# Two attention heads summed in one PSUM bank, one register load per expert tile, one gate transfer per pair of experts, and a new instruction order

## The chip, the cores and the metric

The kernel runs on one core of one Trainium2 chip. A core has five engines that run side by side, each through its own instruction stream: TensorE (PE, matrix products, with its weight loads shown as PEld), VectorE (DVE), ScalarE (ACT), GpSimd (POOL) and SyncE (SP), which here issues nearly all DMA transfers. Matrix products land in PSUM, eight banks of 512 fp32 numbers on each of 128 partitions; everything else on chip lies in SBUF. The metric is device time in microseconds (us) of one execution.

## The reference

Input x has 8 sequences of 512 tokens with 128 features, fp32. Four sublayers follow each other, each wrapped in a residual and a layer normalization without gain:

```python
x = _layernorm(x + _L0_attn_ref(x, ...))   # linear attention, 16 heads, plus an ELU feed forward
x = _layernorm(x + _L0_ffn_ref(x, ...))    # mixture of 8 experts of 64, every expert on every token, top-2 gates
x = _layernorm(x + _L1_attn_ref(x, ...))   # softmax attention, 16 heads of 8, rotary positions
x = _layernorm(x + _L1_ffn_ref(x, ...))    # mixture of 8 experts of 176 (top 2) plus one shared expert
```

The change touches the second, the third and the fourth. The heart of each:

```python
# second: gates of all 8 experts, zero except for the two best
h = gelu(einsum('bsd,edh->bseh', x, w1) + b1)
out = einsum('bse,bsed->bsd', gates, einsum('bseh,ehd->bsed', h, w2) + b2)
# third
attn = softmax(einsum('bhqd,bhkd->bhqk', q, k) / sqrt(8), axis=-1)
out = einsum('bhqk,bhkd->bhqd', attn, v)
# fourth
h = silu((einsum('td,edh->teh', xf, w1) + b1) * (einsum('td,edh->teh', xf, w3) + b3))
y = einsum('te,ted->td', rw, einsum('teh,ehd->ted', h, w2) + b2) + z    # z: the shared expert
```

## The kernel before, in words

**Recorded, then issued in a written order.** The kernel's code doesn't issue instructions as it runs. A recorder (`Schedule`) notes each operation as a numbered piece of work, with what it depends on; groups inside `nc.together()` are one piece. At the end `issue()` emits them in the order of a long tuple of numbers, `ORDER`. Every PSUM tile gets its bank from a string, `BANK_OF`. Each engine then runs its own instructions strictly in that order, and waits where a semaphore isn't there yet. Since an engine is in order, a wait holds up all that stands behind it; on SP this means that a DMA that waits for its data delays every DMA issued after it. The costs in the recorder's calls (such as 0.9, 2.0) are what an offline planner used when it made `ORDER`; they aren't instructions.

**The stages.** First `keys()` makes the sums of the linear attention over all batches (about the first 200 us). Then, batch by batch and interleaved over several batches: `linear_attention_and_ffn`, `first_mixture`, `softmax_attention`, and the last mixture. For the first six batches the last mixture is sorted: `sort` finds each token's two experts, and 8 indirect DMAs per batch (`scatter`, on POOL) put each token's row twice into a DRAM array, ordered by expert. `tiles` then walks over that array, `combine` fetches each token's two results with 8 indirect DMAs (`gather`, POOL). Batches 0 to 4 are one group, cut into 27 tiles of 256 rows; batch 5 is a group by itself, 15 tiles of 128 rows. Batches 6 and 7 run through `dense_mixture`, all experts on all tokens.

**Softmax attention (`softmax_attention`, L1306).** The 16 heads are split into j = 0..3 and g = 0..3, head 4g + j. For each j, and each quarter kt of the keys, `probabilities` computes the scores of four heads at once (L1330, four matmuls side by side in PE's rows) and two exponentials on ACT (L1336). `values` (L1340) then multiplies them by the values: four matmuls side by side in PE's columns (L1342), head g writing PSUM rows 32g to 32g+31. The stationary operand is a window of 32 columns of `vv`, where each head has 8 columns of values and one column of ones, which gives the softmax's denominator; what the window holds beyond these nine (columns of the next heads) ends in rows that nobody reads. After four kt the bank of j is complete: DVE copies it to SBUF (L1349), four transposes on PE bring it into token order (L1351, the helper is L770), DVE takes the reciprocals of the denominators into `rden` (L1354) and multiplies (L1355). This happens four times a batch, once for each j. `values` runs one step behind `probabilities`. `attention_output` follows, and a check of `rden` (L1376, L1377), which sends the kernel to a general path, not taken here, where a sum is out of range.

**Gates of the first mixture (`first_mixture`, L1168).** The gates, [8 experts, 512 tokens], go to DRAM (L1211) and come back spread over partitions: for each of four tiles c, 64 partitions have the gates of expert 2c and 64 those of 2c+1. The helper `spread` (L1041) issues one DMA per expert (L1047), so two a tile and 8 a batch. DVE multiplies the hidden values by them (L1226) ahead of the matmuls L1233.

**Tiles of the sorted mixture (`tiles`, L1770).** Which expert a tile belongs to, and which row it starts at, is known only at run time. DVE writes both for all tiles into a small integer array `listed`, experts in one row and first rows in the other. Per tile SP needs them three times: to fetch the expert's weights (L1684), to fetch the rows (L1689), and to store the result (L1696). Each time `number` (L1676) loads the number from SBUF into an SP register (L1677), and the DMA takes its address from it. The weights have a ring of three buffers, so the weights of a tile can be fetched once the tile three before it is done. The tile's work: transposes (L1818), three hidden matmuls (L1824), `gated` on ACT and DVE, the output matmuls (L1832), and DVE's L1837.

Small tiles come from `tiny`, most with two buffers in turn.

Of the kernel before, what the change touches and what calls it, by code (L numbers as in the profile page):

```python
# [31 lines left out]
ALU = mybir.AluOpType  # L32
# [3 lines left out]
P = 128  # L36
B, N, D = 8, 512, 128
NT = N // P
# [5 lines left out]
V1 = (H2 - 1) * (HD2 + 1) + 32  # L44
# [42 lines left out]
    1, 4, 45, 687, 47, 32, 54, 686, 0, 13, 3, 5, 10, 15, 69, 7, 679, 70, 2, 39, 72, 82, 71, 53, 18, 50, 55, 680,  # L87
    52, 73, 683, 49, 35, 684, 4504, 20, 27, 66, 34, 12, 9, 67, 30, 11, 81, 28, 68, 8, 74, 23, 41, 90, 6, 75, 126,
    46, 78, 48, 127, 83, 76, 77, 89, 80, 85, 91, 682, 128, 79, 129, 86, 98, 51, 87, 97, 84, 105, 106, 88, 99, 133,
    681, 92, 94, 134, 93, 135, 100, 17, 40, 138, 33, 1281, 96, 22, 101, 130, 102, 95, 137, 26, 103, 145, 139, 146,  # L90
    104, 142, 147, 140, 141, 107, 148, 192, 150, 193, 153, 144, 108, 194, 149, 16, 25, 42, 143, 177, 152, 176, 185,
    151, 178, 109, 110, 179, 112, 184, 154, 111, 186, 155, 113, 195, 180, 136, 156, 187, 181, 157, 189, 158, 159,
    182, 188, 161, 183, 196, 160, 190, 197, 162, 204, 191, 205, 173, 212, 163, 206, 164, 198, 65, 200, 199, 172,
    201, 209, 202, 166, 688, 203, 208, 174, 207, 165, 168, 211, 235, 210, 236, 167, 237, 243, 238, 244, 169, 245,
    213, 170, 214, 175, 171, 310, 215, 251, 216, 217, 246, 220, 240, 239, 252, 248, 242, 115, 114, 241, 247, 116,
    219, 255, 218, 256, 264, 257, 231, 263, 221, 258, 222, 265, 249, 223, 232, 225, 254, 271, 250, 259, 260, 233,
    267, 261, 268, 262, 227, 266, 272, 224, 294, 270, 226, 269, 295, 273, 229, 296, 303, 311, 302, 312, 228, 304,
    299, 230, 305, 298, 630, 297, 306, 661, 274, 24, 234, 275, 301, 38, 278, 253, 316, 29, 314, 279, 31, 21, 315,
    300, 43, 277, 19, 307, 631, 317, 313, 290, 324, 308, 14, 651, 323, 44, 309, 327, 632, 325, 654, 318, 660, 328,
    280, 643, 320, 326, 633, 291, 319, 370, 329, 638, 282, 321, 284, 292, 281, 283, 322, 285, 331, 276, 330, 355,  # L100
    286, 354, 363, 356, 362, 357, 371, 287, 372, 364, 288, 359, 365, 289, 430, 639, 358, 655, 634, 332, 293, 360,
    366, 333, 361, 334, 367, 335, 339, 383, 368, 635, 340, 689, 384, 37, 369, 647, 337, 375, 376, 385, 342, 338,
    341, 377, 350, 379, 378, 343, 386, 380, 351, 344, 336, 391, 374, 387, 381, 346, 56, 382, 685, 348, 352, 388,
    414, 390, 345, 389, 415, 347, 416, 422, 490, 663, 431, 636, 423, 650, 432, 659, 392, 353, 424, 393, 394, 349,
    419, 395, 417, 664, 399, 641, 418, 36, 425, 400, 646, 426, 421, 373, 436, 411, 427, 420, 435, 665, 396, 429,
    648, 443, 437, 428, 444, 397, 447, 445, 402, 398, 446, 401, 410, 440, 434, 451, 438, 439, 404, 441, 412, 452,
    403, 442, 448, 406, 449, 405, 450, 475, 453, 474, 407, 476, 482, 491, 483, 492, 454, 493, 484, 413, 666, 455,
    456, 477, 653, 645, 408, 657, 494, 479, 485, 409, 667, 478, 662, 460, 575, 487, 480, 652, 459, 486, 481, 458,
    471, 649, 495, 489, 457, 496, 503, 668, 488, 470, 504, 461, 505, 462, 497, 472, 500, 498, 507, 506, 464, 499,
    463, 501, 465, 502, 467, 511, 508, 466, 509, 534, 510, 535, 512, 542, 536, 513, 543, 514, 544, 468, 516, 539,  # L110
    545, 469, 546, 515, 537, 519, 547, 517, 538, 520, 473, 540, 118, 518, 531, 120, 541, 122, 124, 117, 119, 121,
    548, 123, 521, 125, 530, 550, 549, 523, 551, 522, 552, 553, 532, 525, 555, 554, 573, 559, 692, 558, 693, 557,
    524, 570, 533, 556, 697, 694, 569, 64, 526, 574, 595, 576, 583, 571, 527, 560, 695, 572, 584, 577, 528, 578,
    585, 696, 579, 529, 637, 580, 708, 669, 698, 707, 581, 699, 582, 728, 700, 709, 727, 710, 59, 586, 712, 587,
    729, 711, 588, 701, 562, 589, 713, 561, 590, 60, 730, 564, 690, 714, 747, 715, 748, 591, 749, 592, 716, 702,
    597, 600, 596, 593, 703, 131, 563, 594, 61, 565, 717, 62, 567, 63, 691, 132, 750, 566, 704, 57, 602, 568, 58,
    705, 706, 601, 605, 718, 751, 598, 723, 719, 720, 722, 599, 721, 731, 724, 732, 610, 725, 733, 603, 734, 604,
    735, 607, 606, 726, 736, 772, 752, 608, 737, 743, 753, 909, 742, 640, 612, 670, 744, 754, 738, 611, 745, 755,
    613, 615, 739, 614, 740, 741, 912, 756, 913, 776, 746, 773, 757, 762, 914, 763, 916, 764, 915, 917, 620, 758,
    765, 759, 777, 918, 910, 927, 642, 609, 760, 766, 928, 919, 761, 656, 621, 929, 920, 767, 433, 931, 774, 921,  # L120
    930, 658, 768, 922, 932, 769, 947, 933, 948, 934, 778, 935, 770, 949, 923, 936, 622, 771, 937, 775, 616, 779,
    950, 623, 617, 924, 968, 780, 925, 618, 781, 938, 967, 625, 619, 782, 926, 911, 951, 786, 783, 939, 943, 940,
    785, 941, 784, 969, 787, 942, 788, 789, 970, 952, 944, 791, 953, 796, 793, 954, 955, 792, 627, 798, 626, 794,
    797, 956, 799, 801, 628, 957, 795, 629, 800, 802, 803, 806, 790, 958, 808, 807, 804, 959, 809, 805, 822, 960,
    810, 961, 671, 962, 811, 945, 815, 814, 812, 813, 819, 816, 818, 817, 963, 820, 672, 821, 824, 673, 826, 964,
    825, 823, 830, 827, 971, 829, 828, 674, 831, 833, 972, 834, 837, 832, 838, 835, 836, 965, 839, 840, 675, 644,
    841, 946, 844, 973, 845, 676, 842, 1316, 843, 974, 966, 975, 846, 848, 982, 847, 677, 983, 849, 867, 984, 850,
    851, 869, 976, 868, 871, 993, 997, 977, 870, 873, 872, 852, 992, 874, 985, 996, 875, 853, 978, 854, 979, 858,
    1323, 1317, 855, 986, 980, 678, 856, 859, 1324, 981, 1320, 994, 1325, 1319, 857, 988, 860, 1321, 861, 987, 862,
    863, 1338, 989, 1322, 864, 990, 865, 1326, 866, 1327, 624, 1335, 991, 876, 1328, 998, 995, 1339, 877, 999,  # L130
    1000, 1001, 882, 1334, 1340, 1318, 1329, 880, 1336, 879, 883, 1337, 1355, 1354, 878, 1002, 1341, 886, 1006,
    1342, 1004, 885, 1003, 1005, 1007, 884, 1374, 1008, 1330, 1356, 1016, 887, 1343, 1021, 881, 1018, 1357, 1011,
    1344, 888, 1013, 1012, 889, 1331, 1017, 1009, 890, 1014, 1345, 891, 1023, 1332, 1015, 1346, 1019, 1304, 1010,
    1020, 1022, 1333, 1026, 892, 1028, 1349, 1347, 1027, 1375, 894, 896, 893, 895, 1350, 900, 898, 899, 897, 1376,
    901, 1358, 1348, 902, 1024, 903, 1029, 1025, 906, 1042, 905, 1377, 1351, 1030, 904, 1359, 907, 1031, 1244,
    1129, 1035, 1360, 1130, 1133, 1033, 1032, 1034, 1037, 1039, 1038, 1036, 1143, 1046, 1134, 1040, 1044, 1041,
    1045, 1131, 1043, 1144, 1135, 1352, 1047, 1137, 1051, 1145, 1055, 1361, 1049, 1147, 1132, 1378, 1053, 1050,
    1379, 1048, 1054, 1052, 1058, 1369, 1057, 1056, 1723, 1059, 1136, 1370, 1060, 1146, 1371, 1138, 1353, 1362,
    1372, 1148, 1399, 1363, 1061, 1139, 1727, 1065, 1364, 1064, 1373, 1141, 1063, 1400, 1726, 1380, 1062, 908,
    1066, 1728, 1404, 1403, 1149, 1068, 1067, 1365, 1151, 1087, 1150, 1729, 1091, 1140, 1088, 1089, 1152, 1092,  # L140
    1093, 1090, 1142, 1742, 1094, 1741, 1069, 1170, 1095, 1381, 1153, 1366, 1070, 1072, 1382, 1071, 1731, 1154,
    1367, 1073, 1368, 1730, 1074, 1390, 1075, 1078, 1076, 1389, 1079, 1077, 1383, 1080, 1081, 1082, 1083, 1391,
    1732, 1384, 1084, 1743, 1392, 1085, 1086, 1744, 1155, 1097, 1385, 1156, 1096, 1393, 1100, 1386, 1157, 1401,
    1158, 1733, 1387, 1724, 1734, 1099, 1159, 1161, 1103, 1388, 1160, 1171, 1162, 1098, 1163, 1395, 1105, 1394,
    1164, 1165, 1102, 1106, 1396, 1101, 1169, 1405, 1735, 1166, 1397, 1167, 1192, 1736, 1168, 1172, 1398, 1175,
# [446 lines left out]
def kernel(ctx: ExitStack, tc: tile.TileContext, i: dict, out: bass.AP):  # L592
# [120 lines left out]
    wqf = keep("wqf", [P, HM])  # L713
    rtT = keep("rtT", [P, 2 * E1])

    rdens = Ring([keep(f"rden{n}", [P, 4, NT, 4]) for n in range(2)])
    bad = keep("bad", [P, B])


# [19 lines left out]
    for v in vvs.places:  # L739
        nc.gpsimd.memset(v, 1.0)  # L740
# [1274 lines left out]
```

## Time and profile before

| what | value |
|---|---|
| device time, median of 9 runs (lowest to highest) | 1135.38 us (1130.17 to 1140.62) |
| the profiled execution, device time | 1133.91 us |
| its span in the profile | 1131.8 us, 17007 instructions |
| PE's granted clock, mean | 0.978 |
| eviction copies L1349 | 32 of 0.686 us |
| transposes of one 128x128 block, all of L770 | 320 |
| value matmuls L1342 | 1024 records of 128x32 by 128x512 |
| exponentials of the softmax L1336 | 256 of 1.026 us |
| loads of a number into an SP register L1677 | 126 |
| DMA issues L1047, SP | 100, of which 64 in the first mixture and 36 in the dense one |
| indirect DMAs on POOL L1662, L1670 | 48 and 48, about 1.0 us each |

The page's second part shows where each engine works, in 40 slices of 28.3 us (tenths of busy time; PEclk is the granted clock):

```profile
PE   7999999998888999998999999999899888789995
...
DVE  3866666787898856889677787577679765765785
```

PE's row is full nearly everywhere; the last quarter has the thinnest part. How to read the group lines in the rest of this document: line of the code, engine, operation, what it writes and reads, shapes, how often; then busy time in total and the mean of one in ns; then the engine's idle time just before these instructions, and what ended most of it.

### The profile page before, as it was taken

How to read it: one execution, taken by the hardware profiler on the slowest of the kernel's cores; microseconds unless marked ns; L12 is line 12 of the kernel's file. 1: busy time of each engine (PE TensorE's matmuls, PEld its weight loads, DVE VectorE, ACT ScalarE, POOL GpSimd, SP SyncE). 2: the span in 40 equal slices, each digit the busy share in tenths (PEclk: the TensorE clock that was granted, in tenths of full speed). 3: DMA queues.
4: the chain of work that ended last, by engine and by line, in shares of the span. 5: the costliest groups of instructions: out<-in, count | busy, mean ns of one | idle time of the engine just before them, and what ended most of it. 6: DMA issues, size and time to landing. Idle time of an engine off the chain costs nothing.

```text
span 1131.8 us, 17007 instructions
## 1 busy us (share of the span) xinstructions
PE 1042.1 (92%) x5753; PEld 594.7 (53%) x5753; DVE 824.9 (73%) x1977; ACT 716.3 (63%) x971; POOL 425.2 (38%) x382
## 2 busy tenths in 40 slices
PE   7999999998888999998999999999899888789995
PEld 4444444575565445565455554444587646453553
DVE  3866666787898856889677787577679765765785
ACT  2434445565546898646788777697566765678554
POOL 0232343133262623237653354354124212433463
PEclk9999999999999999999999999899899999899998
DMA  6114470252314321025232233131357855552532
GB/s 199 43 34 152 153 242 12 103 203 72 108 56 141 118 88 57 1 85 186 71 136 75 76 133 96 62 129 33 115 172 237 257 153 179 188 166 86 149 112 77
DMA packets 103374, 134.55 MB, mean 119 GB/s; under 512 B 19650, under 2 KB 60669, under 8 KB 103281
## 3 DMA queue, kind: packets, MB, share of 16 engines
q1 hardware_dynamic: 99905, 126.55, 35.3%
q0 software_dynamic: 3072, 6.30, 2.0%
q8 instruction: 47, 0.77, 0.3%
q10 hardware_dynamic: 304, 0.56, 0.2%
q14 instruction: 46, 0.38, 0.1%
HBM read 81.93 MB, written 54.43 MB: 120 GB/s over the span
## 4 chain that ended last, share of the span: by engine, by line
PE 67%; DVE 13%; ACT 8%; DMA 4%; issue 4%; POOL 1%; another core or an unknown queue 1%; SPq 1%; POOLq 0%; ACTq 0%; DVEq 0%
PE ps L1342 9%; PE ps L857 5%; PE ps L818 5%; PE ps L828 5%; PE ps L1330 4%; PE ps L1110 4%; PE ps L1072 4%; ACT scratch L1336 3%; PE ps L1062 3%; PE ps L770 3%; PE ps L1824 2%; PE ps L1233 2%; PE ps L1102 2%; PE ps L1832 2%; PE ps L1137 2%
## 5 line engine op out<-in xcount | busy, mean ns | idle before, releaser
L1336 ACT ACTIVATE scratch<-ps 128x1024 f32<-128x1024 f32 x256 | 248.6, 1026 | 68.5 <-PE ps L1330 60.7
L1342 PE MATMUL ps<-scratch,vv 128*32 128x512 f32 x1024 | 140.5, 608 | 0.9 <-ACT scratch L1336 0.9
L1086 POOL TENSOR_TENSOR scratch<-scratch 128x1024 f32<-128x1024 f32 x32 | 65.6, 2049 | 113.5 <-ACT scratch L1083 92.3
L1330 PE MATMUL ps<-qx,kx 32*128 32x512 f32 x512 | 73.4, 499 | 21.6 <-ACT scratch L1336 8.4
L823 ACT ACTIVATE scratch<-ps 128x1024 f32<-128x1024 f32 x32 | 32.4, 1021 | 77.6 <-PE ps L818 71.5
L1330 PEld LDWEIGHTS ps<-qx,kx 32*128 32x128 f32 x512 | 29.6, 183 | 90.7 <-ACT scratch L1336 34.8
L1110 PEld LDWEIGHTS ps<-scratch 128*128 128x128 f32 x512 | 60.3, 192 | 13.9 <-ACT scratch L1106 7.2
L1110 PE MATMUL ps<-scratch 128*128 128x128 f32 x512 | 64.4, 279 | 2.7 <-ACT scratch L1106 2.7
L1072 PE MATMUL ps<-wqf,scratch 128*128 128x512 f32 x128 | 65.8, 614 | 1.1 <-ACT scratch L1106 1.1
L1062 PE MATMUL ps<-wq,scratch 128*128 128x512 f32 x128 | 64.7, 617 | 2.0 <-ACT scratch L1067 1.2
L818 PE MATMUL ps<-scratch 128*128 128x512 f32 x128 | 62.5, 610 | 0.7 <-ACT scratch L810 0.4
L857 PE MATMUL ps<-scratch,x_sb 128*128 128x512 f32 x128 | 62.0, 597 | 0.0
L1670 POOL DMA_INDIRECT scratch<-x_d,slots x48 | 48.4, 1008 | 34.3 <-DVE scratch L1851 19.3
L828 PE MATMUL ps<-scratch 128*128 128x512 f32 x128 | 61.2, 598 | 0.0
L1017 POOL TENSOR_TENSOR f_ln_rs<-f_ln_ve,nhalf 128x4 f32<-128x4 f32 x24 | 26.5, 1102 | 89.5 <-DVE f_ln_ve L1015 57.2
L1824 PE MATMUL ps<-scratch 128*128 128x256 f32 (+1 forms) x252 | 54.7, 353 | 4.7 <-DMA scratch<-w_d 3.3
L1662 POOL DMA_INDIRECT x_d<-scratch,slots x48 | 49.1, 1023 | 22.2 <-DVE slots L1736 12.1
L825 DVE TENSOR_REDUCE scratch<-scratch 128x16 f32<-128x1024 f32 x32 | 38.2, 1213 | 25.7 <-ACT scratch L823 25.5
L770 PE MATMUL ps<-ident,scratch 128*128 128x128 f32 x224 | 38.2, 293 | 11.8 <-DVE scratch L1349 6.4
L1824 PEld LDWEIGHTS ps<-scratch 128*128 128x128 f32 x252 | 40.8, 194 | 15.6 <-issue 3.6
L1709 ACT ACTIVATE scratch<-scratch 128x512 f32<-128x512 f32 (+2 forms) x48 | 29.5, 615 | 28.8 <-DVE scratch L1706 14.7
L1106 ACT COPY scratch<-ps 128x1024 f32<-128x1024 f32 x32 | 32.5, 1015 | 23.4 <-PE ps L1102 22.0
(292 smaller groups left out, 2475.4 us busy)
## 6 DMA issues: line engine op xcount, KB each, us to landing
halves_d<-scratch SPq DMA_DIRECT2D x32, 512.0 KB
scratch<-w_d SPq DMA_DIRECT2D x42, 386.0 KB
x_d<-scratch SPq DMA_DIRECT2D x27, 512.0 KB
scratch<-g_d SPq DMA_DIRECT2D x68, 128.0 KB
kx<-halves_d SPq DMA_DIRECT2D x32, 256.0 KB
qx<-halves_d SPq DMA_DIRECT2D x32, 256.0 KB
scratch<-z_d SPq DMA_DIRECT2D x8, 520.0 KB
kvo_d<-scratch SPq DMA_DIRECT2D x8, 512.0 KB
```

Of the source, the lines that this page charges most:

```text
L770: nc.tensor.transpose(dst_ps[:, t * P : (t + 1) * P], src[:, t, :], ident)
L818: nc.tensor.matmul(kp_ps[:, a, :], xT[:, t * P : (t + 1) * P], wk[:, a * 512 : (a + 1) * 512], start=True, stop=True,)
L828: nc.tensor.matmul(dp_ps[:, a, :], xT[:, t * P : (t + 1) * P], wkf[:, a * 512 : (a + 1) * 512], start=True, stop=True,)
L857: nc.tensor.matmul(xp_ps[:, a, :], x_of(b)[:, t, :], ek[:, t, a * 512 : (a + 1) * 512], start=(t == 0), stop=(t == NT - 1),)
L1062: nc.tensor.matmul(qp[:, a, :], xT[:, t * P : (t + 1) * P], wq[:, a * 512 : (a + 1) * 512], start=True, stop=True,)
L1072: nc.tensor.matmul(dp[:, a, :], xT[:, t * P : (t + 1) * P], wqf[:, a * 512 : (a + 1) * 512], start=True, stop=True,)
L1086: nc.gpsimd.tensor_tensor(pr, eq, zr[:, 0:HM], ALU.mult)
L1110: nc.tensor.matmul(at_ps[:, 0:D], qnT[:, c, :], kvo[:, c, :], start=(c == 0), stop=(c == 7))
L1330: nc.tensor.matmul(halves[g // 2][:, g % 2, :], kx[quarter, kt * P : (kt + 1) * P], qx[quarter, :], start=True, stop=True, tile_position=( ...
L1336: nc.scalar.activation(pr[:, 2 * a : 2 * a + 2], sc, AF.Exp, scale=1.0 / math.sqrt(HD2))
L1342: nc.tensor.matmul(av[32 * g : 32 * g + 32, :], vv[:, kt, head_columns(4 * g + j)], pr[:, g, :], start=(kt == 0), stop=(kt == NT - 1), til ...
L1824: nc.tensor.matmul(to, w[:, c : c + P], xf, start=True, stop=True)
```

## The change

Five parts.

1. *Two heads in one bank.* Each pair of neighbouring heads (j even, j odd) has 27 columns of `vv`: values and ones of the first, nine zeros, values and ones of the second. The window of the even head begins at its values, that of the odd head nine columns ahead of its own, at the zeros. So the matmuls of the even head give rows 0 to 8 its sums and add zeros to rows 9 to 17, those of the odd head the other way round, and eight steps (two j, four kt) accumulate in one bank. Copy, transposes, reciprocal and multiplication come once per pair.
2. *One gate transfer per tile* of the first mixture: one DMA whose source has two rows, each read 64 times.
3. *One load per tile* of the sorted mixture: `listed` holds expert and first row side by side, one instruction loads both into SP registers, and the three DMAs of the tile use them. The rows are fetched first now, since that step loads the numbers; the weights come after it. The store begins with a no-op on SP.
4. *Fewer buffers*: `vv` is wider (216 columns a key tile in place of 167), and `rden`, `ln_st`, `lg`, `ge`, `cnt`, `base` and `listed` have one buffer in place of two.
5. *Order anew*: `ORDER` and `BANK_OF` are other numbers throughout. Not shown.

```diff
-V1 = (H2 - 1) * (HD2 + 1) + 32
+V1 = H2 // 2 * 3 * (HD2 + 1)
...
-    rdens = Ring([keep(f"rden{n}", [P, 4, NT, 4]) for n in range(2)])
+    rdens = Ring([keep("rden", [P, 2, NT * 4, 2])])
...
-    vvs = Ring([keep(f"vv{n}", [P, NT, V1]) for n in range(2)])
+    vvs = Ring([keep(f"vv{n}", [P, NT * V1 + 23]) for n in range(2)])
+    def by_pair(v):
+        return v[:, 0 : NT * V1].rearrange("p (t u a e) -> p t u a e", t=NT, a=3, e=HD2 + 1)
     for v in vvs.places:
-        nc.gpsimd.memset(v, 1.0)
+        nc.gpsimd.memset(v, 0.0)
+        for a in range(2):
+            nc.gpsimd.memset(by_pair(v)[:, :, :, 2 * a, HD2], 1.0)
...
         for c in range(FC):
             gr = tile2("e_t")
-            spread(gr, g1_d[b], c * P, M)
+            nc.sync.dma_start(gr, g1_d[b, 2 * c : 2 * c + 2].unsqueeze(1).to_broadcast([2, M, N]))
...
-    def head_columns(h):
-        return slice(h * (HD2 + 1), h * (HD2 + 1) + 32)
+    def head_columns(h, t, second=0):
+        at = t * V1 + h // 2 * 3 * (HD2 + 1) + (2 * (h % 2) - second) * (HD2 + 1)
+        return slice(at, at + 32)
...
-                        av[32 * g : 32 * g + 32, :], vv[:, kt, head_columns(4 * g + j)], pr[:, g, :],
-                        start=(kt == 0), stop=(kt == NT - 1), tile_position=(0, 32 * g),
+                        av[32 * g : 32 * g + 32, :], vv[:, head_columns(4 * g + j, kt, j % 2)], pr[:, g, :],
+                        start=(j % 2 == 0 and kt == 0), stop=(j % 2 == 1 and kt == NT - 1), tile_position=(0, 32 * g),
                     )
-            if kt < NT - 1:
+            if j % 2 == 0 or kt < NT - 1:
                 return
...
-            trv = tr.rearrange("p (t g e) -> p t g e", g=4, e=32)
-            rd = rden[:, j]
+            trv = tr.rearrange("p (t e) -> p t e", e=32)[:, :, 0 : 2 * (HD2 + 1)]
+            trv = trv.rearrange("p t (a e) -> p t a e", a=2)
+            rd = rden[:, j // 2]
             nc.vector.reciprocal(rd, trv[:, :, :, HD2])
             nc.vector.tensor_tensor(
-                at5[:, :, :, j, :], trv[:, :, :, 0:HD2],
-                rd.unsqueeze(3).to_broadcast([P, NT, 4, HD2]), ALU.mult,
+                at5[:, :, j // 2], trv[:, :, :, 0:HD2], rd.unsqueeze(3).to_broadcast([P, NT * 4, 2, HD2]), ALU.mult,
             )
...
-                if kt == 0:
+                if kt == 0 and j % 2 == 0:
                     av = psb("av", brief=False)
...
-    def fetch_tokens(group):
-        def go(x, rows_d, first):
+    def fetch_tokens(group, tile):
+        def go(x, rows_d, pair):
             r = ROWS[group]
-            inst = tc.nc.sync.dma_start(x, rows_d[bass.ds(number(first, SLOTS[group] - r), r)].rearrange("(t p) d -> p t d", p=P))
+            _, numbers[tile] = tc.nc.values_load_multi_w_load_instructions(
+                pair, engines=[mybir.EngineType.SP], min_val=0, max_val=SLOTS[group] - r,
+                skip_runtime_bounds_check_because="made of counts of tokens that add up to no more than the slots",
+            )
+            inst = tc.nc.sync.dma_start(x, rows_d[bass.ds(numbers[tile][1], r)].rearrange("(t p) d -> p t d", p=P))
             apart("fetch", group, inst, [("scatter", group)])
...
+    def store_tokens(group, tile):
+        def go(rows_d, y, _):
+            tc.nc.sync.nop()
...
-        listed = tiny("m", [P, 2, 5 * E2], "listed", 2, mybir.dt.int32)
-        nc.vector.tensor_scalar(listed[:, 0, 0:most], expert, float(E2 - 1), None, ALU.min)
-        nc.vector.tensor_scalar(listed[:, 1, 0:most], at, float(tr), None, ALU.mult)
+        listed = tiny("m", [P, 5 * E2, 2], "listed", 1, mybir.dt.int32)
+        nc.vector.tensor_scalar(listed[:, 0:most, 0], expert, float(E2 - 1), None, ALU.min)
+        nc.vector.tensor_scalar(listed[:, 0:most, 1], at, float(tr), None, ALU.mult)
...
-            nc.do("sync", fetch_weights, (w,), (w_d, which), 0.9, 2.0)
-            nc.do("sync", fetch_tokens(group), (x,), (rows_d, first), 0.9, 2.0, ("tiles", group))
+            nc.do("sync", fetch_tokens(group, tile), (x,), (rows_d, listed[0:1, j]), 0.95, 2.0, ("tiles", group))
+            nc.do("sync", fetch_weights(tile), (w,), (w_d, listed[0:1, j]), 0.5, 2.0)
+            nc.works[-1].before.add(tile)
```

## The prediction

> **What bounds the kernel now.** I read the page first: the share of the engines and the chain of waits.
>
> ```profile
> PE 1042.1 (92%) x5753; PEld 594.7 (53%) x5753; DVE 824.9 (73%) x1977; ACT 716.3 (63%) x971; POOL 425.2 (38%) x382
> ...
> PE 67%; DVE 13%; ACT 8%; DMA 4%; issue 4%; POOL 1%; another core or an unknown queue 1%; SPq 1%; POOLq 0%; ACTq 0%; DVEq 0%
> ```
>
> TensorE (PE) is busy for 92% of the span and is two thirds of the chain that ended last. DVE and ACT have a quarter to a third of the span to spare, and SP's queue is 1% of the chain. So an instruction taken from PE should shorten the run, and one taken from DVE or SP only where that engine is what PE waits for.
>
> Then the windows by stage, because a share of the whole mixes stages:
>
> ```profile
> 500.00:815.00 315.00, 300.58 (x1813) 160.24 (x1814) 230.01 (x623) 234.50 (x301) 150.24 (x160) 0.97 0.31 100
> 815.00:1010.00 195.00, 165.97 (x1081) 121.46 (x1080) 142.33 (x413) 125.12 (x215) 58.13 (x60) 0.96 0.64 196
> ```
>
> (Columns: stretch, length, busy PE, PEld, DVE, ACT, POOL, granted clock, DMA share, GB/s.) From 500 to 815 us PE stands still for only 14.4 us of 315. From 815 to 1010 us, where the 42 expert tiles run, it stands still for 29.0 of 195, and the DMA engines are twice as busy. PE sets the pace in the first, DMAs and SP share in it in the second.
>
> Third, the groups by line and shape (busy us, mean ns | idle time before, who ended it), for the lines that the change touches:
>
> ```profile
> L770 PE MATMUL ps<-ident,scratch 128*128 128x128 f32 x224 | 38.2, 293 | 11.8 <-DVE scratch L1349 6.4 <-ACT scratch L1026 3.4 <-issue 1.5
> L1226 DVE TENSOR_TENSOR scratch<-scratch 128x512 f32<-128x512 f32 x32 | 25.9, 824 | 12.1 <-DMA scratch<-g_d 9.0 <-issue 3.1
> L1349 DVE COPY scratch<-ps 128x512 f32<-128x512 f32 x32 | 22.0, 686 | 28.5 <-PE ps L1342 16.6 <-remote 9.3 <-issue 2.5
> L1837 DVE SCALAR_TENSOR_TENSOR scratch<-scratch,ps 128x256 f32<-128x256 f32 x27 | 11.2, 416 | 7.4 <-PE ps L1832 4.9 <-issue 2.1
> L1355 DVE TENSOR_TENSOR scratch<-ps,rden 128x128 f32<-128x128 f32 x32 | 9.0, 282 | 0.4
> L1354 DVE RECIPROCAL rden<-ps 128x16 f32<-128x16 f32 x32 | 8.0, 249 | 25.1 <-PE ps L770 18.9 <-PE ps L1330 6.2
> ```
>
> **Part 1, two heads in one bank.** The value matmuls (L1342) stay as many. What goes is every second eviction: 16 copies L1349, 16 groups of four transposes (L770 called from L1351), 16 reciprocals and 16 multiplications; the 16 that stay of the last two are twice as wide. One group in the timeline:
>
> ```profile
> 641.03 0.67 DVE L1349 COPY scratch<-ps 128x512 f32<-128x512 f32 x1
> ...
> 642.18 0.66 PE L770 MATMUL ps<-ident,scratch 128*128 128x128 f32 x4
> ...
> 642.77 0.16 PEld L1342 LDWEIGHTS ps<-scratch,vv 128*32 128x32 f32 x8 [0.17 <-issue]
> ```
>
> From the first transpose to PE's next instruction is 0.59 us: that, not the 293 ns that one transpose is shown to last, is what the group costs PE. I took this step for all 32 groups in the timeline: 17.5 us. The 16 groups of even j, which go, hold 9.0 us, and PE stood still 4.8 us just ahead of them (3.2 of it at 911, 1.2 at 558). PE term: at least 64 transposes x 0.109 us (the step inside a group) = 7.0; at most 9.0 + 4.8 = 13.8; I take 9.0, for most of that idle time ends with a stall that hits DVE and ACT too (below), and will fall on another instruction.
>
> On DVE: 16 x 0.686 = 11.0 of copies; multiplications 32 x 0.282 = 9.0 become 16 x 0.416 (L1837, the nearest row with 256 elements) = 6.7; reciprocals 8.0 become 4.0 to 8.0. Together 13 to 17 us. Hidden: DVE is 27% idle, and it counts only where PE waits for the copy, which is in the 13.8. If that cover were gone, all 17 would count. The wider multiplication makes the end of each batch's attention 0.13 us later, 8 x 0.13 = 1.1 at worst; nothing, since the halved work before it is worth more.
>
> The Trainium skill (TensorE: Matmul & The Clock Gate, Part 4: PE-mode transpose) gives about 275 ns for a 128x128 transpose inside a kernel; this trace's 293 ns of one agrees. By it the 64 would be worth 17.6 us, but the trace shows four overlapping in 0.59 us, and the measurement decides.
>
> **Part 2, gates of two experts by one transfer.** Per batch, 8 issues L1047 become 4. SP saves 32 x 0.53 us (their mean in the trace) = 17 us, if one issue of two rows costs what one of one row does; two would be the upper bound, and then nothing is saved. The bytes are the same (256 KB a tile). PE feels only the first tile of a batch, whose landing DVE L1226 waits for:
>
> ```profile
> 299.27 4.30 DMA scratch<-g_d
> ...
> 486.09 4.29 DMA scratch<-g_d
> ...
> 625.11 3.67 DMA scratch<-g_d
> ...
> 920.74 3.79 DMA scratch<-g_d
> ```
>
> Four of the eight batches have it on the chain. One issue less ahead of the second half of the tile is 0.53 each, so 4 x 0.53 = 2.1 at most on the chain as it stands; 0 to 4.2 for eight; I take 1.5.
>
> **Part 3, a tile's numbers read once.** SP ran 126 loads L1677, mean 0.311 us (median 0.272), 39.2 us; 42 stay. A load of two numbers isn't in the trace: between one load (0.272) and two (0.544), so 11.4 to 22.8 us stay and 16 to 28 go. [...] In 815 to 1010 us SP had 108 us of work (62.8 issuing, 34.7 in loads, 10.8 in register work) and 34.0 of waiting in 195. So it is not the bound, but it can be late, and lateness there is soon felt: from the issue of a tile's weights (L1684) to its first matmul (L1824) is 4.9 us in the median of 42, and a landing takes
>
> ```profile
> 881.36 4.01 DMA scratch<-w_d
> ...
> 909.85 3.52 another core or an unknown queue
> ...
> 958.30 5.82 another core or an unknown queue
> ...
> 1005.48 3.26 DMA scratch<-w_d
> ```
>
> 3.3 to 4.0. The two stretches of 3.5 and 5.8 us are of one kind: POOL runs eight indirect DMAs in a row, and DVE, ACT and PE stand still; in the second SP's instructions slow to 0.7 us apiece. Fewer SP instructions there may shorten them. Term: 0 to 9.3 us; I take 1.5, since nothing takes the POOL run away (96 indirect DMAs before and after).
>
> The Trainium skill (Runtime: NRT & Kernel Launch, Instruction fetch mechanics) speaks against this part: about 200 ns a register even in bulk, so one load of two numbers would cost two. By it SP would go from 126 x 0.2 to 84 x 0.2 and save 8.4 us, not 16 to 28. No row here shows a load of two.
>
> **Part 4, what waits anew.** A tile's tokens are now fetched ahead of its weights, since they bring the number; L1689 can wait for PE to free an x buffer (8.3 us in 5 cases), and behind it on SP stand the weights, and behind those PE. One buffer instead of two for several small tiles, rden and the list: all are written by DVE, mostly after DVE's own reads, and the list's 15 rewritten entries have been loaded long before. Nothing, 0 to 2 us. Zeros in vv: a slightly larger memset and four narrow ones on POOL at the start, where POOL is 38% busy; nothing.
>
> **Part 5, the order.** I compared the built programs. In PE's order, counted by the trace's own steps, the first tile matmul stands behind 701 us of PE work before and 696 after, the last value matmul behind 886 and 880, the end behind 944 and 937. It is the same plan with 7 us taken out, not a new one. Of 128 score groups, 49 had less than 2.5 us of other PE work (two exponentials and their handovers) before their values, now 43. So order anew is 0, with PE's idle time as its scale: a tenth of 76.8 us, 7.7 either way.
>
> **Sum** against the profiled execution: 9.0 + 1.5 + 1.5 = 12.0, so the span goes from 1131.8 to 1119.8. That execution took 1133.9 with what lies around the span, 1.5 under the median of the nine runs, 1135.4; from the median I forecast **1123.4 us**.
>
> **Rivals.**
> *A stall goes too.* The 9.3 us of the two unknown waits and the 4.8 ahead of the removed transposes vanish with the smaller SP load: 1123.4 - 7.8 - 4.8 = 1110.8. For: both lie where SP has most to do. Against: POOL's run of eight stays.
> *PE's time turns into waits.* PE is in order, ACT keeps 716 us of work, and L1330 already waits for L1336; if three quarters of the 12 return as waits for exponentials, 1132.4, no change that can be told. Against: PE has only 14 us of idle time in the 315 us where half of the attention lies.
> *Slower: weights late.* With tokens ahead, each tile's weights are issued later. The slack is 4.9 - 4.0 = 0.9 us; from there on each tile pays. At 1.5 us later, 42 x 0.6 = 25, less 12: 1148.6; it decides from 1.2 us on (42 x 0.3 = 12.6). For: L1824 waits for w_d now (3.3 us). Against: in the new order tokens stand two to four tiles ahead, and SP has two loads a tile fewer.
>
> **How the numbers follow.** A measurement of this kernel can tell about 0.3% (3.4 us) from no change. Forecast 0.56, both stalls 0.14, waits 0.13, slower 0.17. Faster is 0.56 + 0.14 = 0.70, same 0.13, slower 0.17. Range: all terms at their upper bounds, 13.8 + 4.2 + 7.4 = 25.4, give 1110; on the other side into the slower rival as far as 1138, which leaves out its larger half and a few hundredths below. The forecast's own range is 1115 to 1131 (7.7 either way).
>
> **What would show it.** L770 with 64 fewer, L1349 and L1354 at 16, PE's busy time 9 to 18 us less (it counts the shown lengths), the chain's g_d pieces about 0.5 us shorter, SP's loads at 42 with a mean between 0.27 and 0.54, and the issue-to-matmul time of tiles still near 4.9. I'd be wrong if PE's idle time grew by as much as its work shrank, or if L1824 waited for w_d in many tiles.

## Result and profile after

The changed kernel takes 1246.1 us (median of 20 runs, 1239.6 to 1253.6) where the kernel before takes 1133.8 (62 runs): 1.0999 of before, with a 95% interval of 1.0977 to 1.1021. It is slower by 10%, and the prediction had 1123.4.

The page of the changed kernel: the span, the engines, and then, of the picture in 40 slices, PE and its granted clock (here as below, "..." stands for lines left out).

```profile
span 1244.9 us, 16659 instructions
...
PE 1066.5 (86%) x5689; PEld 605.5 (49%) x5689; DVE 804.4 (65%) x1929; ACT 715.2 (57%) x971; POOL 429.2 (34%) x386
...
PE   8999999985876999587799699599859987878995
...
PEclk9999999998898999898899699899889996999998
```

The work is what the change says: PE has 64 instructions fewer (5753 before), DVE 48 fewer (1977). The span grew by 113.1 us. PE's time outside its work went from 1131.8 - 1042.1 = 89.7 to 1244.9 - 1066.5 = 178.4, so 88.7 of the 113.1 are PE's idle time. The other 24.4 are work that lasts longer although it is less of it: the mean granted clock fell from 0.978 to 0.931, and most of PE's dips in the picture have dips of the clock beneath them.

Next the groups by line and shape, those that answer to the prediction's (busy us, mean ns | idle before, who ended it):

```profile
L771 PE MATMUL ps<-ident,scratch 128*128 128x128 f32 x160 | 26.9, 290 | 12.1 <-ACT scratch L1027 6.5 <-DVE scratch L1349 5.2 <-issue 0.4
...
L1227 DVE TENSOR_TENSOR scratch<-scratch 128x512 f32<-128x512 f32 x32 | 21.9, 691 | 137.8 <-DMA scratch<-g_d 137.8
...
L1349 DVE COPY scratch<-ps 128x512 f32<-128x512 f32 x16 | 11.0, 685 | 16.2 <-PE ps L1342 11.4 <-remote 4.6
...
L1356 DVE TENSOR_TENSOR scratch<-ps,rden 128x256 f32<-128x256 f32 x16 | 6.7, 420 | 0.3
...
L1355 DVE RECIPROCAL rden<-ps 128x32 f32<-128x32 f32 x16 | 5.7, 353 | 3.6 <-PE ps L771 3.0 <-ACT scratch L1336 0.6
```

Everything that the removed evictions should change has changed. What stands out is L1227, the multiplication by the gates (L1226 before): it waited 9.0 us for the gates and now waits 137.8. The waits say how often, and who stands behind it (waiter <- awaited: us, times, longest):

```profile
DVE scratch L1227 <- DMA scratch<-g_d: 137.8, 27, 9.1
...
PEld ps L1234 <- DVE scratch L1227: 29.0, 8, 9.9
PE ps L1234 <- DVE scratch L1227: 27.2, 8, 9.7
...
POOL scratch L1173 <- DVE scratch L1227: 24.1, 1, 24.1
...
PE ps L1063 <- DVE scratch L1083: 19.1, 2, 14.3
```

DVE waits for 27 of the 32 gate tiles, 5 us each in the mean. In one batch, the timeline (start, length, engine, line):

```profile
510.25 0.29 SPq L1212 DMA_DIRECT2D g_d<-gT  x1
...
511.73 3.85 SPq L1226 DMA_DIRECT2D scratch<-g_d  x3
...
515.68 5.48 SPq L1869 DMA_DIRECT2D scratch<-xT_d  x1
519.36 0.69 DVE L1227 TENSOR_TENSOR scratch<-scratch 128x512 f32<-128x512 f32 x1 [3.72 <-DMA scratch<-g_d]
...
521.82 0.58 SPq L1226 DMA_DIRECT2D scratch<-g_d  x1
524.71 0.69 DVE L1227 TENSOR_TENSOR scratch<-scratch 128x512 f32<-128x512 f32 x1 [4.66 <-DMA scratch<-g_d]
...
530.75 3.75 PE L1063 MATMUL ps<-wq,scratch 128*128 128x512 f32 x4 [14.67 <-DMA scratch<-xT_d]
...
536.67 0.69 DVE L1227 TENSOR_TENSOR scratch<-scratch 128x512 f32<-128x512 f32 x1 [8.71 <-DMA scratch<-g_d]
```

Three tiles are issued between 511.7 and 515.6, the fourth at 521.8. The first two are used at 519.4 and 524.7; the multiplication at 536.7 waits on the semaphore of the fourth, and the third, which landed at 530.0, is used after it, at 537.6. The transfer that follows the first three on SP, xT_d, takes 5.48 us to issue, and PE stands still for 14.67 us until it has landed. The DMA view of 508 to 535 us, in 40 slices of 0.675 us, says why (busy share of the 16 engines in tenths, then GB/s):

```profile
DMA  0000100011111111111177931111111111128411
GB/s 0 0 0 0 24 0 0 21 49 52 52 52 49 52 33 24 49 55 49 52 115 240 382 137 52 49 49 49 52 52 49 49 49 49 55 88 243 170 55 49
```

While gates alone move, the row shows one tenth of the engines busy and mostly 49 to 52 GB/s. The packets, counted one by one in these stretches, are about 25 a microsecond, of 2 KB and 84 ns each: 25 x 0.084 = 2.1 engines. So 256 KB take 5.2 us, and four tiles 21 us one behind the other. The semaphores say the same: besides one update a microsecond after the issue, the trace has two landings for a gate tile (519.26 and 519.27 us for the first one), and it has sixteen for xT_d, 14 of them by 523.8 us and the last two at 530.6, behind the gates. The peak in the middle is xT_d and a write to xs_d, issued at 521.3, on the other engines.

Summed over the eight batches, it was 48.1 us from the first to the fourth multiplication before, and it is 143.6 now.

### The profile page after: what moved, and what is told of

Same layout as the page of the kernel before. It is cut to its first block, busy times and chain, and to the rows that moved or that the text cites. A ratio compares the mean times of both kernels' runs of the same rounds, so it can differ in the third digit from the quotient of the medians.

```text
span 1244.9 us, 16659 instructions
## 1 busy us (share of the span) xinstructions
PE 1066.5 (86%) x5689; PEld 605.5 (49%) x5689; DVE 804.4 (65%) x1929; ACT 715.2 (57%) x971; POOL 429.2 (34%) x386
## 5 line engine op out<-in xcount | busy, mean ns | idle before, releaser
L1336 ACT ACTIVATE scratch<-ps 128x1024 f32<-128x1024 f32 x256 | 248.7, 1027 | 101.4 <-PE ps L1330 90.8
L1342 PE MATMUL ps<-scratch,vv 128*32 128x512 f32 x1024 | 145.9, 630 | 2.3 <-ACT scratch L1336 1.4
L1227 DVE TENSOR_TENSOR scratch<-scratch 128x512 f32<-128x512 f32 x32 | 21.9, 691 | 137.8 <-DMA scratch<-g_d 137.8
L1063 PE MATMUL ps<-wq,scratch 128*128 128x512 f32 x128 | 69.9, 653 | 35.3 <-DVE scratch L1083 19.1
L824 ACT ACTIVATE scratch<-ps 128x1024 f32<-128x1024 f32 x32 | 32.6, 1021 | 76.7 <-PE ps L819 72.7
L1111 PEld LDWEIGHTS ps<-scratch 128*128 128x128 f32 x512 | 61.3, 193 | 15.3 <-issue 6.9
L1234 PE MATMUL ps<-mw,scratch 128*128 128x128 f32 x256 | 44.7, 324 | 27.2 <-DVE scratch L1227 27.2
L1830 PE MATMUL ps<-scratch 128*128 128x256 f32 (+1 forms) x252 | 57.5, 367 | 2.0 <-DMA scratch<-w_d 1.6
L1670 POOL DMA_INDIRECT scratch<-x_d,slots x48 | 49.3, 1027 | 26.0 <-issue 11.1
L1068 ACT ACTIVATE scratch<-ps 128x1024 f32<-128x1024 f32 x32 | 32.7, 1023 | 38.0 <-PE ps L1063 38.0
L1234 PEld LDWEIGHTS ps<-mw,scratch 128*128 128x128 f32 x256 | 40.3, 235 | 29.0 <-DVE scratch L1227 29.0
```

The lines of the kernel that those rows point to most:

```text
L1063: nc.tensor.matmul(qp[:, a, :], xT[:, t * P : (t + 1) * P], wq[:, a * 512 : (a + 1) * 512], start=True, stop=True,)
L1111: nc.tensor.matmul(at_ps[:, 0:D], qnT[:, c, :], kvo[:, c, :], start=(c == 0), stop=(c == 7))
L1234: nc.tensor.matmul(op[:, sl], hT[:, c, t * P : (t + 1) * P], mw2[:, c, :], start=False, stop=(c == FC - 1),)
L1336: nc.scalar.activation(pr[:, 2 * a : 2 * a + 2], sc, AF.Exp, scale=1.0 / math.sqrt(HD2))
L1342: nc.tensor.matmul(av[32 * g : 32 * g + 32, :], vv[:, head_columns(4 * g + j, kt, j % 2)], pr[:, g, :], start=(j % 2 == 0 and kt == 0), st ...
L1830: nc.tensor.matmul(to, w[:, c : c + P], xf, start=True, stop=True)
```

## Experiments

Each run was compared with the kernel before on its own chip. There were three chips. Before takes 1104.1 us beside the first run with two transfers, each tile fetched twice, two copies and eight copies; 1128.4 beside the second run with two transfers, the evictions twice, three loads and half the evictions; 1130.4 beside the other four. So ratios are compared, and times in the expectations are to be read against 1133.8. The ratios with their 95% intervals are not the quotients of these medians; for the runs near 1 the two differ by up to 0.0014, or 1.6 us.

**Two transfers a tile in the new order.**

```diff
-            nc.sync.dma_start(gr, g1_d[b, 2 * c : 2 * c + 2].unsqueeze(1).to_broadcast([2, M, N]))
+            with nc.together():
+                for a in range(2):
+                    nc.sync.dma_start(gr[a * M : (a + 1) * M, :], g1_d[b, 2 * c + a].partition_broadcast(M))
```

> The changed kernel, but each gate tile is fetched by two transfers of 64 partitions in the place of the one of 2 x 64; order, banks, buffers and everything else stay. Theory A (few engines): the one transfer runs on two DMA engines. In the changed kernel's trace the DMA engines move 25 packets of 2 KB a microsecond, 84 ns each, while only such a transfer runs: 25 x 0.084 = 2.1 engines, 50 GB/s, so 256 KB take 5.2 us, and four tiles 21 us one behind the other. With two transfers the time falls to 1115 to 1135 us (the sum of the prediction gives 1123), the four multiplications of a batch spread over 5 to 8 us instead of 13.5 to 20.3, and DVE waits for g_d 5 to 20 us in all instead of 137.8. Theory B (the order, the single buffers or the tokens ahead of the weights are at fault, and the wait for the gates is only where it shows): 1230 to 1255 us.

1101.6 us against 1104.1: 0.9972 (0.9943 to 1.0001). The spread of a batch's four multiplications is 5.3 to 8.0 us, 54.2 in all. The group by line, with its mean, shows the wait gone:

```profile
L1229 DVE TENSOR_TENSOR scratch<-scratch 128x512 f32<-128x512 f32 x32 | 22.5, 713 | 16.3 <-DMA scratch<-g_d 12.5 <-ACT scratch L1338 3.8
```

137.8 us have become 12.5, by this edit alone. The order, the single buffers and the tokens ahead of the weights are all still in this kernel, so theory B falls.

**One transfer a tile in the order of before.** The two works of a tile in the order of before are meant to share one function (`gates_once`, not shown): the first to be issued is to fetch the whole tile, and the second to do nothing.

```diff
-            spread(gr, g1_d[b], c * P, M)
+            for a in range(2):
+                nc.do("sync", gates_once(gr), (gr[a * M : (a + 1) * M, :],), (g1_d[b, 2 * c : 2 * c + 2],), 0.6, 2.0)
```

> The kernel before, its order and banks, with the gate tile fetched by one transfer of 2 x 64 partitions in the place of the first of its two; the second becomes a no-operation. Theory A (few engines): the whole loss appears here too: the first-to-fourth multiplication of eight batches took 48.0 us before and 143.6 after, 96 us more, and the span grew by 113; so 1215 to 1250 us. Theory B (order, buffers, tokens first): 1130 to 1140 us, as before.

1.3123 (1.3076 to 1.3170): far beyond both. The edit did not do what the expectation says. The function was made anew for each work, so neither knew of the other and both fetched the tile: eight transfers of 256 KB a batch on two engines. It is a run with the suspected cost doubled, and the wait shows it: 352.4 us at the multiplication, 302.5 from first to fourth. Done as meant, with one function for both works (`once = gates_once(gr)` ahead of the inner loop, and `once` in its place):

> The kernel before, in its order, with the gate tile fetched by one transfer of 2 x 64 partitions. In the earlier run of this edit both works issued the transfer, so each tile was fetched twice on two engines (512 KB a tile) and the time was 1.31 of before; here the second work is a no-operation. Theory A (two engines, order not at fault): 256 KB a tile at 50 GB/s as in the changed kernel, so about its loss without the gain of the other parts: 1.08 to 1.14 of before. Theory B (the new order or the single buffers have a share in the loss): below 1.06.

1.1037 (1.0984 to 1.1089), inside theory A's range, and no different from the whole change's 1.0999. Page and waits of this run:

```profile
PE 1081.8 (87%) x5753; PEld 621.2 (50%) x5753; DVE 820.6 (66%) x1977; ACT 717.0 (57%) x971; POOL 423.3 (34%) x382
...
DVE scratch L1239 <- DMA scratch<-g_d: 127.1, 28, 10.0
```

PE and DVE have all the instructions of before, and the wait is there. The one transfer is enough for the whole loss.

**One transfer with more rows in its source.** The gates are written to DRAM two or eight times over, so that a tile's source is 4 rows for 32 partitions each, or 16 rows for 8 each; still one transfer, the same bytes and packets. The edit for two:

```diff
-    g1_d = tc.dram_tile([B, E1, N], F32, name="g1_d")
+    g1_d = tc.dram_tile([B, E1, 2, N], F32, name="g1_d")
...
-        nc.sync.dma_start(g1_d[b], gT1[0:E1])
+        nc.sync.dma_start(g1_d[b], gT1[0:E1].unsqueeze(1).to_broadcast([E1, 2, N]))
...
-            nc.sync.dma_start(gr, g1_d[b, 2 * c : 2 * c + 2].unsqueeze(1).to_broadcast([2, M, N]))
+            rows_of = g1_d[b, 2 * c : 2 * c + 2].rearrange("e k n -> (e k) n")
+            nc.sync.dma_start(gr, rows_of.unsqueeze(1).to_broadcast([4, 32, N]))
```

> The changed kernel, still one transfer a tile, but the gates are written to DRAM twice over (32 KB instead of 16), so that a tile's source is 4 rows, each spread over 32 partitions: the same 256 KB and the same 128 packets of 2 KB. Theory A, if the number of engines is that of the outermost rows: four engines, 100 GB/s, 2.6 us a tile, 10.5 us for four; most of the stall goes, 1125 to 1175 us, and the packets run at 50 a microsecond. Theory C (one transfer that spreads several rows is slow whatever its outermost count): 1235 to 1255 us, 25 packets a microsecond.

> As the run with two copies, with eight: the gates are written eight times over (128 KB instead of 16), and a tile's source is 16 rows, each spread over 8 partitions. Theory A: all 16 engines, so 1115 to 1140 us, as with two transfers, less one issue of about 0.5 us a tile and plus a longer write of the gates ahead of them. Theory C: 1235 to 1255 us.

Two copies: 1.0387 (1.0341 to 1.0433), a little above theory A's upper end (1175 / 1133.8 = 1.036). Eight copies: 1.0147 (1.0120 to 1.0174), above its end of 1.005. With two copies, the DMA view from 280 to 310 us, where the gates follow one another from 290 us on (slices of 0.75 us):

```profile
DMA  7303887000002002223994222222222200000000
GB/s 311 115 0 111 316 273 16 0 0 0 0 14 30 0 0 66 98 101 126 319 287 117 87 98 98 98 112 101 93 90 104 87 14 0 0 0 0 0 0 0
```

Twice the engines and about twice the rate, 87 to 117 GB/s where gates alone move: four engines for four rows. Here too the landings in the trace agree: four for a gate tile with two copies, sixteen with eight copies, sixteen for each half with two transfers. In one table, with the sum over eight batches from the first to the fourth multiplication, and that from the issue of the gates' write to the first multiplication:

| kernel | rows of a tile's source | first to fourth, us | write to first, us | ratio to before |
|---|---|---|---|---|
| before | 2 transfers, 64 partitions each | 48.1 | 49.8 | 1 |
| two transfers, new order | the same | 54.2 | 49.3 | 0.9972 |
| eight copies | 16 | 53.3 | 66.9 | 1.0147 |
| two copies | 4 | 85.0 | 68.8 | 1.0387 |
| changed | 2 | 143.6 | 82.7 | 1.0999 |

Theory C falls: it is not that one transfer serves two experts, but how many rows stand outermost. With 16 rows the tiles follow one another as fast as with two transfers. What eight copies still lose is in the fourth column, (66.9 - 49.3) / 8 = 2.2 us a batch ahead of the first tile. There the kernel writes 128 KB instead of 16, and the first gate transfer, which needs that write, is issued 4.5 us behind the issue of the write instead of 1.5 (medians of eight batches); the expectation had allowed too little for the write.

The Trainium skill says this outright (DMA: Bandwidth & Descriptors, Why a DMA increments its semaphore by 16 and not by 1): a transfer runs on the largest number of engines up to 16 that divides the slowest dimension, other than 1, of both its sides. Its Rules for kernel authors add that an outermost dimension of c below 16, a leading broadcast for example, confines the transfer to at most c engines. The runs agree for 2, 4 and 16 rows by the number of landings, for 2 and 4 also by the rates, and for 16 by the spread of the multiplications.

**What the other parts are worth.** With the gates mended, 3 us of gain are left where the prediction's other terms add up to 10.5. The two-transfer kernel was run again, beside three others.

> The kernel of the run with two transfers a tile once more, beside the next three, so that they are compared with it on one chip. It was 0.9972 of the kernel before, 3.1 us faster, with an interval that just touches no change. The prediction's sum without its term for the gates is 12.0 - 1.5 = 10.5 us. Theory P (the removed evictions are worth their 9, and the new order takes most of it back) and theory Q (the removed evictions were worth little, the order nothing) both expect 0.994 to 1.000 again; below 0.992 the sum would stand and the first run was low.

0.9949 (0.9920 to 0.9979): 1128.4 x 0.0051 = 5.8 us. Both runs of this kernel together lie near 4.5.

In the next, the removed evictions' work is done again in the kernel with two transfers: copies and transposes twice, reciprocals and multiplications in two halves (the halves are not shown).

```diff
-            nc.vector.tensor_copy(avs, av)
+            with nc.together():
+                for _ in range(2):
+                    nc.vector.tensor_copy(avs, av)
...
-            transpose4(tr, tok(avs))
+            with nc.together():
+                for n in range(2 * NT):
+                    t = n % NT
+                    nc.tensor.transpose(tr[:, t * P : (t + 1) * P], tok(avs)[:, t, :], ident)
```

> The kernel with two transfers a tile, in which each pair of heads is copied out of its bank twice, transposed twice, and its reciprocals and multiplications are done in two halves: 16 copies, 64 transposes, 16 reciprocals and 16 multiplications more, as many as the change removed. Theory P: 9 us more than the run with two transfers (7 to 14), so 1.003 to 1.010 of the kernel before. Theory Q: 0 to 4 us more, so 0.996 to 1.002.

1.0093 (1.0056 to 1.0130), 0.0144 or 16 us above the run before. Theory P's 7 to 14 lies below that, though within the intervals; theory Q's 0 to 4 does not. The doubled work is also not where the removed work was: each second copy stands between a pair's last value matmul and its transposes. With the second edit of that diff alone, the transposes:

> The kernel with two transfers a tile, with the 16 groups of four transposes done twice, 64 transposes more on PE and nothing else. The prediction's PE term: 9.0 us (7.0 by the step inside a group) above the kernel with two transfers, so 1.001 to 1.006 of before. If the removed transposes lay beside other waits: 0 to 4 us, 0.995 to 1.000. The run with all evictions' work again was 16 us above it; what is left of that is the copies and the other work on DVE.

0.9998 (0.9967 to 1.0029). Above the two runs of the two-transfer kernel (0.9972, 0.9949) that is 2.9 and 5.5 us, so 64 transposes are worth some 4 us, less than the 7.0 of the step inside a group; with the intervals, 7 is not excluded, nor, against the first of the two runs, is nothing. By subtraction, which no run of its own shows, the other 12 of the 16 us are the doubled DVE work, where it was put.

The same part taken out of the kernel before (the wider multiplication is not shown), in its own order, the output then holding the odd head's values twice:

```diff
+            first = len(nc.works)
...
+            if j % 2 == 0:
+                for work in nc.works[first:]:
+                    work.calls = []
```

> The kernel before, in its order, with the copies, transposes, reciprocals and multiplications of heads j = 0 and 2 left out; those of j = 1 and 3 fill both heads' places, so that the multiplication is as wide as in the changed kernel, and the output holds the odd head's values twice. Theory P: 9 us less than before (7 to 14), 0.987 to 0.994. Theory Q: 0 to 4 us less, 0.996 to 1.000.

0.9938 (0.9914 to 0.9963): 7.0 us less, 4.2 to 9.7. This is every instruction that part 1 removes, DVE's with PE's, left out in the old order. It lies at the lower end of theory P.

Three loads a tile again, in the new order (the two places, the weights' likewise):

```diff
-            _, numbers[tile] = tc.nc.values_load_multi_w_load_instructions(
-                pair, engines=[mybir.EngineType.SP], min_val=0, max_val=SLOTS[group] - r,
...
+            at = number(pair[:, 1:2], SLOTS[group] - r)
```

> The kernel with two transfers a tile, with the numbers of an expert tile read by three loads, one ahead of each of its transfers, as before (126 loads instead of 42, no no-operations); tokens stay ahead of the weights. The prediction put the load of two numbers at 1.5 us in the sum (0 to 9.3): 1.5 us more than the run with two transfers (0 to 9). Rival R (SP's loads are hidden in this order too, or a load of two holds its tile up as long as two loads): -3 to +0.5 us.

0.9931 (0.9901 to 0.9960), 2 us less than with one load, with intervals that overlap: rival R's place. And one load in the kernel before, in its order:

> The kernel before, in its order, with a tile's two numbers read by one load and kept (whichever of the two fetches is issued first loads both; the store has a no-operation), two buffers for the list. The prediction's term: 1.5 us less (0 to 9.3), 0.992 to 1.000. Rival R (SP's loads are hidden work): 0.998 to 1.003.

0.9978 (0.9952 to 1.0004): 2.5 us less, from 5.4 less to 0.5 more. It fits the term and no gain alike. Both of the parts together in the order of before:

> The kernel before, in its order, with the evictions of heads j = 0 and 2 left out as in the earlier run (0.9938 there; the output holds the odd head's values twice) and the numbers read by one load. It is the change without its gates and its new order. Sum of the prediction's terms 9.0 + 1.5 = 10.5 us less: 0.991. If its ratio is below that of the two-transfer kernel (0.9949, 0.9972) by more than 0.003, the new order with its single buffers and tokens ahead costs 3 us or more; if they are equal, the order is worth nothing, as predicted, and the parts themselves are worth about 5 us instead of 10.5.

0.9957 (0.9931 to 0.9982), 4.9 us less, 2.0 to 7.8. It lies between the two runs of the two-transfer kernel (0.9949 and 0.9972), so the new order with its single buffers and tokens first is worth nothing that these runs can tell. What the two parts gain together is about 5 us, and the forecast 10.5 lies outside the interval.

The quickest kernel of the study is the changed one with two transfers a tile and three loads (0.9931); it beats the kernel before and the changed one, though it can't be told from the one with two transfers and one load.

## Why the prediction was wrong

**The step that failed is part 2's landing.** The prediction said: "The bytes are the same (256 KB a tile). PE feels only the first tile of a batch", and took the chain's pieces of 3.67 to 4.30 us from rows in which a tile came by two transfers. It bounded the issue of the new transfer and not its movement, although no row of the trace showed a transfer of that shape. The bytes were indeed the same, and an issue was much the same in the median (0.541 us against 0.502; in the mean 0.88 against 0.53, for five of the 32 lasted over 1.5 us). But the tile moved at 50 GB/s, so that it took 5.2 us of moving by itself, and DVE waited for 27 of the 32 tiles, not only for the first of a batch. In place of a term of 1.5 us (0 to 4.2) stands a loss of 10% (1.1037 alone, in the order of before). The kernel before issued the two halves as transfers of 64 partitions each, whose outermost count is 64; the diff shows the outermost count becoming 2, and that was the thing to ask about.

**No rival held it.** The slower rival was the weights of the expert tiles, and they are not late: PE's matmuls waited for w_d 3.3 us before and 1.5 after (L1830, two shapes, 1.2 and 0.3). From the issue of a tile's weights to its first matmul it is 5.2 us in the median, against 4.9. The range's upper end of 1138 rested on that rival alone. The wider of the two shapes, before:

```profile
L1824 PE MATMUL ps<-scratch 128*128 128x256 f32 x162 | 40.4, 385 | 4.2 <-DMA scratch<-w_d 3.3 <-DVE scratch L1303 0.9
```

And after:

```profile
L1830 PE MATMUL ps<-scratch 128*128 128x256 f32 x162 | 43.7, 409 | 1.3 <-DMA scratch<-w_d 1.2
```

Three numbers around the sum were off as well, without a share in the miss. Of the 4.8 us that PE stood still ahead of the removed transposes, the 1.2 at 558 stand ahead of four other transposes, of x_sb, which stay; so 3.6, and 12.6 instead of 13.8 as part 1's upper end. The lower end of the range takes 7.4 us for part 3, whose own bound was 9.3; with that it would be 1108 instead of 1110. And PE's idle time, the scale for the order, is 89.7 us by the page and not 76.8.

**Part 1** was right in kind. The counts are as predicted, the wider multiplication costs 6.7 us as worked out from L1837's row, and the reciprocals 5.7, inside 4.0 to 8.0. PE's busy time at one clock (0.978) is 1037.8 us with the transposes twice and 1029.9 with eight copies: 7.9 us for 64 transposes, near the 7.0 of the step inside a group. That is rough, since before, with as many matmuls as the first and the same clock, shows 1042.1. In time the part gave 7.0 us in the old order (4.2 to 9.7), the lower bound of its term. The forecast's 9.0 lies inside the interval, the 13.8 with the waits ahead of the removed groups outside.

**Part 3** was too hopeful about SP. In the changed kernel SP's loads, with one other among them, take 25.8 us in 43 instead of 39.6 in 127: 13.8 us gone, below the range of 16 to 28. A load of two numbers is 0.488 us in the median, 1.8 times the 0.272 of one. The rule that the prediction set against this part (the Trainium skill, Runtime: NRT & Kernel Launch, Instruction fetch mechanics, some 200 ns a register in bulk) would give 0.4 for two, an estimate, which is nearer to the measurement than the price of one. The page says it of register loads that the runtime puts in; those measured here read the list in SBUF. The time of the kernel moved by 2.5 us less in one order and 2 more in the other, both not told from nothing; the term of 1.5 stands unrefuted but not shown, and the runs agree with the reason for its smallness, that SP is not the bound.

**Parts 4 and 5** were costed at nothing and the runs agree: 0.9957 without the new order, 0.9949 and 0.9972 with it. So without its gates the change would have gained some 5 us instead of 10.5, about 0.4%. The two sized terms were too large together; which of them by how much, the intervals don't tell.

**The signs named** did show it. "I'd be wrong if PE's idle time grew by as much as its work shrank" was met many times over: the idle time grew by 88.7 us, and PE's busy time, forecast to fall by 9 to 18 us, rose by 24.4. The g_d wait is the first line of the waits.

## What to carry to other kernels

Equal bytes are not equal time: when a transfer's shape changes, look at its outermost count on both sides, because a transfer that spreads two rows ran on two DMA engines here, at 50 GB/s. Two transfers with 64 partitions outermost cost one more issue of half a microsecond, and the four multiplications of a batch then lay 5.3 to 8.0 us apart instead of 13.5 to 20.3. A price that no row of the trace shows needs a bound for every stage of the operation, its movement as well as its issue, and a first guess at who is queued behind it.

## What the hardware showed besides

- A slow transfer holds others up. xT_d, issued behind three gate tiles, had 14 of its 16 landings by 523.8 us and the last two at 530.6, behind the gates; PE started on it at 530.75.
- SP's issues suffered too. Those that lasted over 1.5 us were 7 before (14.4 us in all), 19 after (69.0 us; the one of xT_d 5.48) and 24 with one transfer a tile in the order of before (85.3 us); with the two transfers a tile there are 4 (8.7 us). What holds an issue up is not shown: the run that fetched every tile twice has only 13 (30.4 us).
- Where PE waited more, its mean granted clock was lower: 0.978 before (92% busy), 0.931 after (86%), 0.869 in the run with every gate tile fetched twice (74%). The work lasted longer as well, 1073.8 us in that run for the same matmuls that last 1042.1 before, but not in step with the clock: with one transfer a tile in the order of before it is 1081.8 us at 0.926. So a wait can cost more than its own length; a rule for how much does not follow from these runs.
- The same program ran 1101.6 us on one chip and 1123.8 on another (granted clock 0.988 and 0.974 in the profiled executions), a larger step than any gain looked for here. Only runs beside the kernel before on the same chip tell such gains.
